# A row of zeros in a place of its own, two groups of keys ahead of the fill, and the fill behind the keys' loads

## The chip, the cores and the metric

One core of one Trainium2 chip runs the whole kernel in one launch. The metric is the device time of one execution in microseconds; the time before is 2405.3 us, the median of three runs (2400.01 to 2408.94).

The engines are called as in the profile: PE (matrix products), DVE (vectors), ACT (activations), POOL (GpSimd), SP (the engine that issues most of the transfers). Each runs its own instructions in order, and transfers issued by SP lie in SP's queue in order too.

## What is computed

Two layers of a graph network over 1250 nodes with 512 channels and 40000 edges. Only the first attention matters here. Each edge has a source, a destination and eight biases, one for each head:

```python
s = jnp.einsum('ehd,ehd->eh', q[src], k[dst]) / np.sqrt(D) + att_bias
m = jax.ops.segment_max(s, src, num_segments=n)
p = jnp.exp(s - m[src])
denom = jax.ops.segment_sum(p, src, num_segments=n)
alpha = p / jnp.where(denom[src] == 0, 1.0, denom[src])
agg = jax.ops.segment_sum(alpha[:, :, None] * v[dst], src, num_segments=n)
```

Behind it stand a linear attention over all nodes ("mix") that is added to the first, a feed-forward part, an attention with experts, a graph convolution over the same edges, a second linear attention, and a product-key layer.

## The kernel before

The kernel makes the sparse attention a dense one. A table in DRAM, `adj`, has one row of nine numbers for each pair of source and destination, 1280 x 1280 rows: for each head the sum of the exponentials of the biases of all edges between the two nodes, and how many such edges there are. With it, the attention is computed as a dense one whose exponentials are multiplied by the table (one slab of 128 sources at a time, `load_tile`, L667).

The table is made in three steps.

1. *The fill.* `zeros` (L227) writes zeros into the whole table: one transfer from SP's queue (L229) that reads one short row of zeros in SBUF, `zrow`, again and again, 59.0 MB in all, and one small transfer for some spare rows behind the table (L234). The row `zrow` is set by a memset on POOL (L498). It takes its memory from the pool "fold", under the tag `fwT`, which later holds weights.
2. *The groups of edges.* The key of an edge is source x 1280 + destination. Keys lie in columns of 128 edges, 313 columns. The columns are turned on PE, copied to SBUF by DVE (L275, two buffers) and stored in DRAM (`key_d`, three transfers on ACT's queue, L276). From there `load_keys` (L314, the transfer is L317, on SP's queue) brings nine columns, copied to all partitions, for each group of six columns. The pool of these loads has `KAHEAD` buffers. For each group DVE compares keys with keys (L332 and L342), PE adds up the weights of equal keys (L324), and DVE makes the sums (L349) and the indices (L355) of two batches of three columns.
3. *The scatters.* For each column one indirect transfer with addition (L358), issued by POOL, adds its rows into the table: 313 of them. The scatters come behind the fill, since they add into the same table, and a scatter comes behind those of the batch before last.

`scatter_edges` is a generator: each `pump(1)` writes down the instructions of one group between those of the mix attention. Its first step loads `KAHEAD` groups of keys and calls `zeros`, with the loads that are to land ahead of the fill: those of the keys and those in `early` (the node features and the mix attention's first weights and rows). The fill is then the last entry of `early`; some later loads are told to come behind it. There is one pump behind the first norms (L514), and within the loop over the ten node tiles one at t = 4 and one at t = 9 (L533). Then follow three, twenty, three and ten more by tiles and chunks (L553, L580, L592, L601), more with the projections of the sparse attention (L647, L652), and the rest of the groups at L653.

The order on each engine is made by a scheduler from these lines, with priorities by program order; SBUF comes from pools whose memory is used again when a pool is closed. The pool "edgetmp", which holds the edge weights `wgt`, is closed at L306, and pools that are opened later take its memory, with waits for its last readers. The casts of the weights into `w3` (L297, L299) are such readers.

Of the kernel before, what the change touches and what calls it, by code (L numbers as in the profile page):

```python
# [11 lines left out]
F32 = mybir.dt.float32  # L12
# [10 lines left out]
P = 128  # L23
N = 1250
NP = 1280
NT = NP // P
TAIL = N - (NT - 1) * P
C = 512
KC = C // P
# [9 lines left out]
CH = H + 1  # L39
NKEY = NP * NP  # L40
NROW = NKEY + (G + 1) * P
BIG = 1.0e30
LOWEST = -3.0e38
KAHEAD = 3
WSHIFT = 40.0
CHUNKS = ((0, 512), (512, 512), (1024, 256))
GROUPS = ((0, 4), (4, 4), (8, 2))
# [20 lines left out]
def tile_gps_layers(ctx: ExitStack, tc: tile.TileContext, a, out):  # L68
    nc = tc.nc
# [6 lines left out]
    def ps_mm(shape=(P, 512), name="mm"):  # L76
        return psum.tile(list(shape), F32, tag="mm", bufs=3, name=name)
# [4 lines left out]
    def ps_tr(shape=(P, 512), name="tr"):  # L82
        return psum.tile(list(shape), F32, tag="tr", bufs=2, name=name)
# [68 lines left out]
    def norm_stats(pool, x_t, eps, name):  # L152

        st = pool.tile([P, 6], F32, tag="ln_st", name=name + "st")
        nc.vector.bn_stats(st, x_t)
        mv = pool.tile([P, 2], F32, tag="ln_mv", name=name + "mv")
        nc.vector.bn_aggr(mv, st)
        return mv[:, 0:1], rsqrt(pool, mv[:, 1:2], [P, 1], eps, name)
# [27 lines left out]
    def node_mm(ps, xT, t, w, rows=P):  # L186

        mm(ps[:rows], [(xT[:, c, t * P:t * P + rows], w[:, c, :]) for c in range(xT.shape[1])])

    def nodes_of(t):  # L190
        return TAIL if t == NT - 1 else P
# [9 lines left out]
    adj = dram.tile([NROW, CH], F32, name="adj")  # L201
    key_d = dram.tile([EC, P], F32, name="key_d")
# [17 lines left out]

    s_edge = ctx.enter_context(ExitStack())
    pe = s_edge.enter_context(tc.tile_pool(name="edge", bufs=1, side="right"))
    pkr = s_edge.enter_context(tc.tile_pool(name="edgekr", bufs=KAHEAD, side="right"))
    s_tmp = ctx.enter_context(ExitStack())
    ptmp = s_tmp.enter_context(tc.tile_pool(name="edgetmp", bufs=1, side="right"))

    def zeros(zrow, inputs):  # L227

        ld = nc.sync.dma_start(  # L229
            adj[0:NKEY, :].rearrange("(p r) c -> p (r c)", p=P).rearrange("p (a f) -> p a f", f=1800),  # L230
            zrow[:, None, :].to_broadcast([P, NKEY * CH // P // 1800, 1800]))
        for x in inputs:
            tc.add_manual_dep(ld.ins, x.ins.name, SYNC, reason="inputs come first")
        nc.sync.dma_start(adj[NKEY:NROW, :].rearrange("(p r) c -> p (r c)", p=P), zrow[:, :(G + 1) * CH])  # L234
        return ld
# [30 lines left out]
    if whole < EC:  # L266
        nc.vector.tensor_tensor(keyrel[:, whole:], key[:, whole:], spare[:, :EC - whole], op=OP.subtract)


    for c0 in range(0, EC, P):  # L270
        cn = min(P, EC - c0)
        ps = ps_tr((P, P))
        nc.tensor.transpose(ps[:cn, :], key[:, c0:c0 + cn], ident)
        kt = ptmp.tile([P, P], F32, tag="kt", name="kt", bufs=2)
        nc.vector.tensor_copy(kt[:cn], ps[:cn, :])  # L275
        nc.scalar.dma_start(key_d[c0:c0 + cn, :], kt[:cn])  # L276


    mx = pe.tile([P, H], F32, name="mx")
# [28 lines left out]
    scattered, early = [], []  # L308

    def scatter_edges():  # L310
# [3 lines left out]
        def load_keys(c0):  # L314
            cn = min(G + B, EC - c0)
            kr = pkr.tile([P, (G + B) * P], F32, name="kr")
            ld = nc.sync.dma_start(  # L317
                kr[:, :cn * P],
                bass.AP(tensor=key_d.tensor, offset=key_d.offset + c0 * P, ap=[[0, P], [1, cn * P]]))
            return kr, ld  # L320
# [45 lines left out]
            scattered.append(cur)  # L366

        keys = [load_keys(c0) for c0 in range(0, KAHEAD * G, G)]
        early.append(zeros(zrow, [ld for _, ld in keys] + early))
        keys = [kr for kr, _ in keys]  # L370
        even = None
        for c0 in range(0, EC, G):
# [29 lines left out]
            yield  # L402

    edges = scatter_edges()

    def pump(n):
        for _ in range(n):
            next(edges, None)
# [85 lines left out]
    with (tc.tile_pool(name="mix", bufs=1) as pm, tc.tile_pool(name="mixw", bufs=2) as pw,  # L494
          tc.tile_pool(name="fold", bufs=1) as pfold):
        products = weight_products(pfold)
        zrow = pfold.tile([P, KC, C], F32, tag="fwT", name="zrow").rearrange("p c o -> p (c o)")[:, :1800]
        nc.gpsimd.memset(zrow, 0.0)  # L498
        nc.vector.memset(xn[:, NT - 1, :], 0.0)
        for t in range(NT):  # L500
            n = TAIL if t == NT - 1 else P
# [4 lines left out]
        def row(name):  # L506
            return rows[:, MIX_ROWS.index(name), :]
# [16 lines left out]
        for t in range(NT):  # L524
            ps = ps_mm()
            node_mm(ps, xnT, t, wk)
            nc.vector.tensor_tensor(kp[:, t, :], ps, bke, op=OP.add)
            nc.vector.tensor_scalar_max(kp[:, t, :], kp[:, t, :], eps)
            ps = ps_mm()
            node_mm(ps, xnT, t, wv)  # L530
            nc.vector.tensor_tensor(va[:, t, :, :D], ps.rearrange("p (h d) -> p h d", h=H),
                                    row("mix_bv").rearrange("p (h d) -> p h d", h=H), op=OP.add)
            if t in (4, 9):  # L533
                pump(1)

        kv = pm.tile([P, KC, 2, D + 1], F32, name="kv")
# [56 lines left out]
        for t in range(NT):  # L593
            ps = ps_mm()
            node_mm(ps, hid, t, w2)
            f = pw.tile([P, C], F32, tag="f", name="f")
# [20 lines left out]
    with tc.tile_pool(name="gqkv", bufs=2) as pq:  # L617
# [5 lines left out]
        for t in range(NT):  # L623
            z = pq.tile([P, C], F32, tag="z", name="z")
            m, r = norm_stats(pq, xn[:, t, :], 1e-5, "lnz")
# [226 lines left out]
    def node_norm(pool, t, x_t, eps, name):  # L852

        st = pool.tile([P, 6], F32, tag="nn_st", name=name + "st")
        nc.vector.bn_stats(st, x_t)
        mv = pool.tile([P, 2], F32, tag="nn_mv", name=name + "mv")
        nc.vector.bn_aggr(mv, st)
        w = pool.tile([P, 1], F32, tag="nn_w", name=name + "w")
        nc.vector.tensor_scalar_add(w, mv[:, 1:2], eps)
        s = pool.tile([P, 1], F32, tag="nn_s", name=name + "s")  # L860
        nc.scalar.activation(s, w, AF.Sqrt)
        r = pool.tile([P, 2], F32, tag="nn_r", name=name + "r")
        nc.vector.reciprocal(r[:, 0:1], s)
        nc.vector.tensor_scalar(s, r[:, 0:1], r[:, 0:1], w, op0=OP.mult, op1=OP.mult)
        nc.vector.tensor_scalar(s, s, -0.5, 1.5, op0=OP.mult, op1=OP.add)
        nc.vector.tensor_scalar(r[:, 0:1], r[:, 0:1], s, None, op0=OP.mult)
        nc.vector.tensor_scalar(r[:, 1:2], mv[:, 0:1], r[:, 0:1], -1.0, op0=OP.mult, op1=OP.mult)
        return r

    with tc.tile_pool(name="gff", bufs=1) as pf, tc.tile_pool(name="gffw", bufs=2) as pw:  # L870
# [33 lines left out]
        hTs, early = {}, {}  # L904
        with tc.manual_schedule(engines={nc.tensor.engine, nc.vector.engine, nc.scalar.engine}):
            for t in range(NT + 2):
                if t < NT:
# [7 lines left out]
                    r = node_norm(pw, t, X[:, t, :], 1e-5, "lnf")  # L915
# [24 lines left out]
            for c, (c0, cn) in enumerate(CHUNKS):  # L940
                n = cn // P
                for k, t in enumerate(range(c0 // P, c0 // P + n)):
# [4 lines left out]
                    r = nodes_of(t)  # L947
# [675 lines left out]
    keys = pp.tile([P, 2, 2, NKEYS], F32, name="keys")  # L1623
# [392 lines left out]
```

## Time and profile before

| what | us |
|---|---|
| median of three runs | 2405.3 |
| the profiled execution | 2407.57 |
| its span, first to last instruction | 2405.8 |
| busy in the span: PE | 1982.2 (82%) |
| busy in the span: DVE | 1511.2 (63%) |
| busy in the span: ACT | 811.5 (34%) |
| busy in the span: POOL | 695.8 (29%) |
| the fill, from issue to landing | 146.0 |
| the scatters, first start to last start | 196.7 to 790.5 |
| landing of a load of keys, shortest, median, longest | 3.6, 4.1, 5.6 |
| mean granted clock of PE | 0.904 of full speed |

The share of busy time is a mean over stages that have different limits: the edge stage (up to about 795 us), the sparse attention (to about 1160), and all the rest. A line of a timeline has the start, the duration, the engine, the line of the kernel and the operation; in brackets stand the idle time of the engine just ahead of it and what ended that. "SPq" is SP's instruction queue: its instructions issue transfers, and one that can't yet be issued holds all that are behind it.

### The profile page before, as it was taken

Reading aid. Unit: us, or ns where it says so; the run is one execution under the profiler, and the core shown is the slowest. Engines: PE = TensorE matmul, PEld = TensorE weight load, DVE = VectorE, ACT = ScalarE, POOL = GpSimd, SP = SyncE. Lnnn points to the kernel's source line nnn. Section 1 sums busy time; section 2 is a strip of 40 time slices with the busy share of each in tenths; the row PEclk is TensorE's granted clock in tenths of the full one; section 3 lists DMA queues with packets and bytes.
Section 4 is the critical chain, followed back from the end, with each engine's and each line's share of the span. In section 5 each row is a group of like instructions: output and inputs, shape, how many; then the busy total and the mean of one; then the engine's idle time right before and its main releaser. Section 6 shows DMA issues by size and latency. Waiting matters only on the chain.

```text
span 2405.8 us, 29769 instructions
## 1 busy us (share of the span) xinstructions
PE 1982.2 (82%) x10588; PEld 1179.4 (49%) x10588; DVE 1511.2 (63%) x4838; ACT 811.5 (34%) x1530; POOL 695.8 (29%) x448
## 2 busy tenths in 40 slices
PE   3994898965980499999899999999999999978953
PEld 1453665522440266666544546667445445555521
DVE  8526798599760399999651546655222242589998
ACT  1000111103200277677441166665111132244653
POOL 2006888888888100000000000000000000036665
PEclk9996898965995699999999999999899999989975
DMA  6999565545532665665330100001300101000000
GB/s 259 418 417 286 108 129 125 94 88 122 106 32 3 232 222 188 233 216 194 127 132 26 59 21 1 1 1 31 135 27 27 35 5 66 23 22 10 10 9 17
DMA packets 134336, 255.79 MB, mean 106 GB/s; under 512 B 51757, under 2 KB 90086, under 8 KB 132524
## 3 DMA queue, kind: packets, MB, share of 16 engines
q1 hardware_dynamic: 83728, 240.93, 27.2%
q0 software_dynamic: 46512, 8.02, 7.4%
q10 hardware_dynamic: 3948, 4.95, 0.6%
q8 instruction: 83, 1.36, 0.2%
q14 instruction: 65, 0.53, 0.1%
HBM read 161.05 MB, written 92.80 MB: 106 GB/s over the span
## 4 chain that ended last, share of the span: by engine, by line
PE 45%; DVE 12%; ACT 6%; DMA 2%; issue 1%; SPq 0%; ACTq 0%; DVEq 0%
PE mm L184 21%; PE one L747 4%; PE sc L698 4%; ACT wT L738 3%; PE ag L1400 2%; PE sc L1079 2%; PE av L1133 2%; PE one L737 2%; PE one L1120 2%; DVE sc L1760 2%; DVE ix L1701 1%; DVE ix L1710 1%; DVE rest L1713 1%; DVE v L1707 1%; DVE ex L727 1%
## 5 line engine op out<-in xcount | busy, mean ns | idle before, releaser
L358 POOL DMA_INDIRECT adj<-tot,idx x313 | 499.4, 1595 | 243.1 <-DMA adj<-zrow 147.1
L727 DVE SCALAR_TENSOR_TENSOR ex<-ex,slab 128x1280 f32<-128x1280 f32 x80 | 197.1, 2504 | 0.1
L1331 DVE SCALAR_TENSOR_TENSOR X<-mm,gate,X 128x512 f32<-128x512 f32 x80 | 60.0, 750 | 199.8 <-PE mm L184 199.7
L698 PE MATMUL sc<-kT,q 64*128 64x512 f32 (+1 forms) x480 | 103.6, 555 | 99.0 <-DMA q<-q_d 83.5
L332 DVE SCALAR_TENSOR_TENSOR eq<-kr,key,upto 128x128 bf16<-128x128 f32 (+2 forms) x313 | 145.7, 475 | 48.4 <-PE even L324 25.8
L342 DVE TENSOR_SCALAR_CACHE_REDUCE eqx<-kr,key 128x384 bf16<-128x384 f32 (+1 forms) x312 | 175.7, 599 | 0.0
L1269 POOL MEMSET padded<- 128x128 f32 x3 | 0.5, 204 | 540.2 <-DVE faT L1154 540.2
L738 ACT COPY wT<-one 128x512 f32<-128x512 f32 (+1 forms) x240 | 116.0, 517 | 92.2 <-PE one L737 87.6
L737 PE MATMUL one<-ident,ex 128*128 128x128 f32 x800 | 126.0, 286 | 25.5 <-ACT wT L738 20.6
L184 PE MATMUL mm<-w,hT 128*128 128x512 f32 (+1 forms) x320 | 146.0, 608 | 0.0
L184 PE MATMUL mm<-faT,w 128*128 128x512 f32 (+1 forms) x384 | 140.3, 519 | 0.7 <-ACT bs L1153 0.7
L708 DVE CUSTOM_DVE_ANT_0 ex<-sc,none 128x1280 f32<-128x1280 f32 x80 | 115.8, 1486 | 12.9 <-PE sc L698 11.8
L698 PEld LDWEIGHTS sc<-kT,q 64*128 64x128 f32 x480 | 46.4, 193 | 148.2 <-issue 129.4
L737 PEld LDWEIGHTS one<-ident,ex 128*128 128x128 f32 x800 | 84.7, 141 | 68.4 <-ACT wT L738 48.9
L1093 DVE CUSTOM_DVE_ANT_0 ex<-sc,cmask 128x512 f32<-128x512 f32 (+3 forms) x144 | 72.9, 560 | 66.7 <-PE sc L1079 66.6
L324 PEld LDWEIGHTS <-eq 128*128 128x128 bf16 x625 | 43.4, 102 | 135.5 <-DVE eq L332 91.8
L720 ACT ACTIVATE ex<-ex,low 128x1280 f32<-128x1280 f32 x80 | 104.8, 1361 | 9.9 <-DVE low L713 9.9
L184 PEld LDWEIGHTS mm<-faT,w 128*128 128x128 f32 x384 | 73.4, 192 | 67.1 <-issue 66.1
L684 POOL DMA_DIRECT2D deg_d<-cnt x10 | 8.4, 838 | 336.3 <-ACT attT L754 312.8
L747 PE MATMUL one<-wT,gva 128*64 128x128 f32 x1600 | 101.7, 285 | 3.6 <-ACT wT L738 2.0
L1325 ACT ACTIVATE hT<-mm,cols 128x512 f32<-128x512 f32 (+1 forms) x48 | 29.0, 608 | 218.9 <-PE mm L184 218.9
L184 PEld LDWEIGHTS mm<-w,hT 128*128 128x128 f32 (+1 forms) x320 | 61.6, 193 | 76.8 <-issue 76.8
(493 smaller groups left out, 4155.0 us busy)
## 6 DMA issues: line engine op xcount, KB each, us to landing
adj<-zrow SPq DMA_DIRECT2D x1, 57600.0 KB, 146.0
slab<-adj SPq DMA_DIRECT2D x10, 5760.0 KB, 17.4
kr<-key_d SPq DMA_DIRECT2D x51, 576.0 KB, 4.1
cnt_d<-cnt SPq DMA_DIRECT2D x10, 640.0 KB, 3.0
deg_d<-cnt POOLq DMA_DIRECT2D x10, 640.0 KB, 7.3
adjT<-cnt_d SPq DMA_DIRECT2D x5, 1280.0 KB, 10.7
adj<-tot,idx POOLq DMA_INDIRECT x313, 3.2
fw<-in_L_ffn_W SPq DMA_DIRECT2D x8, 512.0 KB, 3.9
```

Source lines behind the costliest of these rows:

```text
L184: nc.tensor.matmul(ps, lhsT=l, rhs=r, start=i == 0, stop=i == len(pairs) - 1)
L332: nc.vector.scalar_tensor_tensor(eq[:, :n], kr[:, k0 * P:k0 * P + n], key[:, c0 + c:c0 + c + 1], upto[:, B - 1 - c:, :].rearrange("p c x - ...
L342: nc.vector.tensor_scalar(eq[:, :n * P], kr[:, k0 * P:(k0 + n) * P], key[:, c0 + c:c0 + c + 1], None, op0=OP.is_equal, op1=OP.add, accum_o ...
L358: st = nc.gpsimd.indirect_dma_start(out=adj, out_offset=bass.IndirectOffsetOnAxis(ap=idx[:, c:c + 1], axis=0), in_=tot[:, c, :], in_offset ...
L698: nc.tensor.matmul(sc[e][:, d0:d0 + dn], lhsT=q[half(e), m, :], rhs=kT[half(e), m, d0:d0 + dn], start=True, stop=True)
L708: nc.vector.tensor_tensor_reduce(out=ex, in0=sc[e][:, :NP], in1=none, scale=-0.125, scalar=-LOWEST, op0=OP.add, op1=OP.min, accum_out=low[ ...
L720: nc.scalar.activation(exs[e], exs[e], AF.Exp, bias=low[:, e:e + 1], scale=-1.0)
L727: nc.vector.scalar_tensor_tensor(exs[e], exs[e], 1.0, sl[:, :, hd], op0=OP.mult, op1=OP.mult, accum_out=den[:, hd:hd + 1])
L737: nc.tensor.transpose(ps[:, k, :], weights[t, m][e][:, (d0 + k) * P:(d0 + k + 1) * P], ident)
L738: nc.scalar.copy(wT[:, d0:d0 + dn, :], ps[:, :dn])
L747: nc.tensor.matmul(av[half(e), 0, :], lhsT=va[:, d, hd * D:(hd + 1) * D], rhs=turned[e][:, d, :], start=d == 0, stop=d == NT - 1)
L1093: nc.vector.tensor_tensor_reduce(out=exs[e][:, d0:d0 + dn], in0=sc[k][e][:, :dn], in1=cmask[:, NP - n + d0:NP - n + d0 + dn], scale=-0.125 ...
```

## The change

The row of zeros gets a place of its own in the pool "edge", which is opened ahead of all edge work, and its memset stands there, among POOL's first instructions. It has 1600 elements instead of 1800, and the fill names 9216 rows instead of 8192. Two groups of keys are loaded ahead of the fill instead of three, and their pool has two buffers. The fill waits for the three stores of the keys and for `early`, and no longer for the loads of the keys. Of the two pumps in the loop over the node tiles one is left, at the last tile; that group of edges is written down in the last step (L653) instead.

```diff
-KAHEAD = 3
+ZROW = 1600
+KAHEAD = 2
...
     pe = s_edge.enter_context(tc.tile_pool(name="edge", bufs=1, side="right"))
+    zrow = pe.tile([P, ZROW], F32, name="zrow")
+    nc.gpsimd.memset(zrow, 0.0)
     pkr = s_edge.enter_context(tc.tile_pool(name="edgekr", bufs=KAHEAD, side="right"))
...
         ld = nc.sync.dma_start(
-            adj[0:NKEY, :].rearrange("(p r) c -> p (r c)", p=P).rearrange("p (a f) -> p a f", f=1800),
-            zrow[:, None, :].to_broadcast([P, NKEY * CH // P // 1800, 1800]))
+            adj[0:NKEY, :].rearrange("(p r) c -> p (r c)", p=P).rearrange("p (a f) -> p a f", f=ZROW),
+            zrow[:, None, :].to_broadcast([P, NKEY * CH // P // ZROW, ZROW]))
...
+    key_stores = []
...
-        nc.scalar.dma_start(key_d[c0:c0 + cn, :], kt[:cn])
+        key_stores.append(nc.scalar.dma_start(key_d[c0:c0 + cn, :], kt[:cn]))
...
-        early.append(zeros(zrow, [ld for _, ld in keys] + early))
+        early.append(zeros(zrow, key_stores + early))
...
         products = weight_products(pfold)
-        zrow = pfold.tile([P, KC, C], F32, tag="fwT", name="zrow").rearrange("p c o -> p (c o)")[:, :1800]
-        nc.gpsimd.memset(zrow, 0.0)
...
-            if t in (4, 9):
+            if t == NT - 1:
                 pump(1)
```

As the scheduler lays it out, SP's queue then has two key loads, the fill and its small second transfer, two key loads, the weights of L554 and L555, and only then the row of L556 (`gnn_b2`), which stood ahead of the fill. Each later key load keeps its place among SP's transfers. In DVE's order the one reader of `gnn_b2` (L557) moves from the fill's time to behind the fifth group of edges. On POOL only the memset moves, from behind the other early memsets to ahead of four of them.

## The prediction, made before the changed kernel ran

> **What bounds the kernel now.** I read the page's costliest groups first, then the stages, the timelines of SP's and POOL's queues, SP's waits, and the chain at the end of the edge stage. The group of scatters names the place:
>
> ```profile
> L358 POOL DMA_INDIRECT adj<-tot,idx x313 | 499.4, 1595 | 243.1 <-DMA adj<-zrow 147.1
> ```
>
> 313 scatters are busy for 499.4 us, and one single wait before them, for the fill of the table, is 147.1 us. The busy time of each engine by stages (PE, PEld, DVE, ACT, POOL; then granted clock, DMA share, GB/s):
>
> ```profile
> 50.00:196.00 146.00, 117.18 (x445) 64.84 (x445) 55.38 (x196) 7.56 (x23) 0.00 (x0) 0.87 1.01 412
> 196.00:693.00 497.00, 396.81 (x2507) 246.85 (x2508) 416.70 (x1946) 77.61 (x183) 416.47 (x260) 0.84 0.58 119
> 693.00:795.00 102.00, 22.05 (x52) 9.50 (x50) 4.96 (x8) 0.00 (x0) 82.90 (x54) 0.62 0.24 3
> ```
>
> From 50 to 196 the DMA engines are full with the fill; from 196 to 693 POOL scatters; from 693 to 795 only POOL scatters, and PE and DVE have nearly nothing left. POOL's timeline (start, duration, and what ended the idle time before it) gives the two ends of that run, and the row of zeros before it:
>
> ```profile
> 47.95 1.60 POOL L498 MEMSET zrow<- 128x1800 f32 x1 [35.84 <-DVE ln0r L149]
> ...
> 196.70 1.78 POOL L358 DMA_INDIRECT adj<-tot,idx  x1 [147.15 <-DMA adj<-zrow]
> ...
> 790.51 1.54 POOL L358 DMA_INDIRECT adj<-tot,idx  x1 [0.30 <-issue]
> ```
>
> The chain that ended last goes on from the last scatter into the attention: nothing of later stages starts before it.
>
> ```profile
> 790.51 3.52 DMA adj<-tot,idx
> ...
> 794.97 17.42 DMA slab<-adj
> ...
> 812.46 2.46 ACT cnt L682
> ```
>
> So the end of the scatters sets the time of all that follows (2405.8 - 790.5 = 1615 us, untouched by the diff). A scatter comes every 1.85 us (1.545 + 0.30): 312 steps are 577 us, and 196.7 to 790.5 is 593.8. Adding up what each step is above 1.85 gives 16.7; the run has no hole. It starts 1.1 us after the fill lands (49.6 + 146.0 = 195.6). **What moves the fill's end moves the kernel's end, as long as POOL never waits for DVE.** SP's waits and its queue tell why the fill starts at 49.6:
>
> ```profile
> SPq L229 <- POOL zrow L498: 14.9, 1, 14.9
> ...
> SPq L229 <- DMA kr<-key_d: 6.5, 1, 6.5
> ```
>
> ```profile
> 25.56 1.29 SPq L317 DMA_DIRECT2D kr<-key_d  x3
> 27.64 0.33 SPq L124 DMA_DIRECT2D gnn_b<-in_gnn_rows  x1
> 49.58 0.63 SPq L229 DMA_DIRECT2D adj<-zrow  x1
> 50.26 123.39 SPq L234 DMA_DIRECT2D adj<-zrow  x1
> 173.69 6.63 SPq L317 DMA_DIRECT2D kr<-key_d  x3
> ```
>
> SP stood at the fill from 28 on: 6.5 us for the third load of keys, then 14.9 us for the zeros' memset. From 34 to 48 the DMA share is 0.00. The memset stands in memory that the edge weights held, and these are last read by the cast of L297 (45.09 + 2.75 = 47.84).
>
> **The change, step by step.**
>
> *The zeros' row.* It has its own place and is set behind fold_g at about 2.9 us: the wait of 14.9 goes. The memset has 1600 elements instead of 1800: 1.60 x 1600/1800 = 1.42 us, now ahead of POOL's other memsets, which end at 12.11. DVE's first small operation stands beside them until just then:
>
> ```profile
> 4.06 8.07 DVE L518 TENSOR_SCALAR bqe<-cols 128x4 f32<-128x4 f32 x1 [2.07 <-DMA cols<-in_cols]
> ```
>
> So I add 1.42 us to DVE's early path, up to the key copies. The Trainium skill (SBUF — State Buffer, "Who interferes with whom") says that a DVE operation in a two-port mode and a GpSimd instruction hold a shared port pair exclusively, the second waiting for the first. That fits L518; by the page's one-instruction lock it would be free at 10.1, the end of the first memset, where the trace has 12.1.
>
> *What the fill waits for next.* The key stores and the inputs, instead of the key loads and the inputs. The queue's inputs sum to 9.4 MB, and the DMA engines had moved that much by 26.5 to 27 us. Of the key stores, the third copy stood at 25.59 in DVE because it waits until the first store frees its buffer, and was issued at 25.9. With DVE 1.42 later: 27.3. Its landing is not in the trace; the nearest rows are scatters at 2.9 to 3.4 and key loads at 3.6 to 5.6, another key store, beside the full input stream, took 9.4. I take 3.2, since by then the stream has drained: **the fill starts at 30.5**. Bounds: SP reaches it at 27.9; and at most 1.4 behind the 34.5 of the key loads that it waited for before: 36.
>
> *The fill itself.* 59.0 MB in either form, 9216 rows of 6400 bytes for 8192 of 7200. At 412 to 418 GB/s the engines are full, and the input stream with its 2 KB rows moved 432 between 20 and 26 us; so the row size costs nothing that I can see, and 146.0 stays. About 0.5 us is added for the tail of two key loads still in the rings at 30.5 (1.2 MB, issued by 27.9). End: 30.5 + 146.0 + 0.5 = 177.0, against 195.6: **18.6 us earlier**. The Trainium skill (DMA: Bandwidth & Descriptors, "How a descriptor splits into AXI transactions") says that pieces which don't start on 256 bytes cost an extra transaction: 6400 is a multiple of 256, 7200 isn't. A faster fill is among the rivals.
>
> *The third key group and gnn_b2* move behind the fill in SP's queue. gnn_b2's one reader, L557, moves in DVE's order behind the fifth group of edges, far behind that load. Three groups made 18 scatters ready ahead of the fill's end (33 us of POOL); two make 12: 12 x 1.85 = 22.2 us. After the fill, DVE started at 197.13, 1.5 us behind it, and had the next indices at 200.6, 5 us behind it. The 13th scatter is wanted 1.1 + 22.2 = 23.3 us behind it: 18 us to spare. I laid each index (L355) beside its scatter: the smallest lead of all 105 batches is 30.1 us, at the first batch behind the fill, then 32 growing to 67. One group less takes 11.1 off: never under 18. PE and DVE finish what is ahead of the fill's end at 175, with one group less and 1.4 more still about 175: before 177, so their 22 us of standing (DVE 174.5 to 197.1) shrink to some 4.
>
> *Two buffers.* In SP's order each key load keeps its slot and is released by the same event; it is only used one group earlier. For every load I set its issue + 4.6 against the start of the group before its own: 2.5 us to spare at 203.43, 0.6 at the tightest (issue 228.56, group at 233.71), 2.0 near 660, 6.2 through 480 to 560. With the slowest landing, 5.6, one group is 0.4 late, under a lead of 18. Cost: nothing.
>
> *One more group beside the scatters* (its DVE work was done during the fill). The scatters' excess over 1.85 is all ahead of 693, none from 700 to 790 with DVE idle: 16.7/50 = 0.3 us.
>
> Sum: 18.6 - 0.3 = 18.3 us off 2407.6, the profiled execution (span 2405.8 and 1.8 around it): 2389.3. That execution lies 2.3 above the median of 2405.3, so I predict **2387**.
>
> **Rivals.**
> - *The fill waits longer for the stores:* it starts at 36, gain 13: 2392. For it: a key store took 9.4 among the inputs. Against it: the share falls to 0.86 behind 26.
> - *A faster fill* by its other rows: at the best rate near it, the inputs' 432, instead of 418, it takes 146 x (1 - 418/432) = 4.7 us less: 2382. Against it: the engines read full at 418 already. (It is what that page's rule on 256 bytes would make of it.)
> - *The start runs dry:* the groups behind the fill come late, because the pre-fill work of PE ends later than 177. It must end 18 us later to cost anything; at 28 late, 10 are lost: 2397. Against it: PE's work there is one unbroken row of matmuls that ends at 175.
> - *Slower: two buffers starve POOL.* If a key load lands too late in each group, DVE's period of 10.0 us (480 to 560) grows past POOL's 11.9. That takes a landing above 6.2 + 4.6 + 1.9 = 12.7 us. At 14 the period is 13.2: 1.3 x 50 = 65, less the lead of 19 = 46, less the 18.6 gained: 27 slower, 2432. Against it: landings are 3.6 to 5.6.
> - *It doesn't do what it says:* the fill still waits for something at 49: 2405. The row is the first tile of its pool and its memset names no wait in POOL's instruction list; little speaks for it.
>
> **How the numbers follow.** Forecast 0.72; late stores 0.10; faster fill 0.05; dry start 0.05; no move 0.04; starving 0.04. Half a per cent, about what a measurement of this kernel can tell from no change, is 12 us: 2393.3. Faster holds the forecast, the faster fill and half of the late stores, 0.82; same the other half, the dry start and no move, 0.14; slower 0.04. The range goes from a start at 27.9 with the faster fill (2405.3 - 21.2 - 4.7 = 2379) to the late start (2392), widened by 1 and 4 for the spread of the runs (2400 to 2409): 2378 to 2396.
>
> **What would show it.** The fill's DMA issued at 30.5 (27.9 to 36) with a landing near 146; the first scatter near 178 and the last near 772; POOL's wait for the fill about 163 us, since POOL now stands from about 13.5; no scatter waiting on an index; DVE's wait for keys at the fill's end about 4 us instead of 22.6; everything from the first slab on 18 us earlier and otherwise the same. Wrong would be: a fill above 150 us; holes in the run of scatters; key loads that DVE waits for later on.

## The result, and the profile after

The changed kernel takes 2387.25 us, the median of five runs (2384.58 to 2394.72), against 2405.3 for the kernel before (five runs, 2398.38 to 2408.94): a ratio of 0.9925 with an interval of 0.9909 to 0.9941. The forecast was 2387. The profiled execution has a span of 2384.9, 20.9 less than before's.

The group of scatters with its single wait, and the stages, cut at the same events as before's (PE, PEld, DVE, ACT, POOL; granted clock, DMA share, GB/s):

```profile
L362 POOL DMA_INDIRECT adj<-tot,idx x313 | 500.4, 1599 | 260.4 <-DMA kr<-key_d 163.8
```

```profile
32.00:177.00 145.00, 126.22 (x439) 67.42 (x437) 61.96 (x181) 7.43 (x23) 0.00 (x0) 0.92 1.01 412
177.00:675.00 498.00, 395.01 (x2488) 246.41 (x2489) 414.65 (x1925) 77.45 (x183) 417.03 (x260) 0.82 0.59 122
675.00:777.00 102.00, 27.96 (x100) 12.08 (x98) 15.26 (x62) 0.00 (x0) 83.38 (x54) 0.66 0.26 3
```

The three stages have kept their lengths within 1 us, and all of them lie earlier. The third has one more group's work in it (PE 28.0 against 22.1, DVE 15.3 against 5.0). POOL's busy time is the same (500.4, before 499.4), and its wait is longer only because POOL has stood since 13.7. The page of the profile now names a key load as what ended that wait. The scatters wait for several transfers, and the profile has no landing of the fill in this run; in experiment nine, where it has one, the fill lands 144.7 us behind its issue and the first scatter starts 1.3 us later. POOL's timeline shows the ends of the run, and SP's queue and wait show what the fill starts behind:

```profile
2.87 1.44 POOL L225 MEMSET zrow<- 128x1600 f32 x1
...
177.50 1.78 POOL L362 DMA_INDIRECT adj<-tot,idx  x1 [163.82 <-DMA kr<-key_d]
...
772.98 1.55 POOL L362 DMA_INDIRECT adj<-tot,idx  x1 [0.30 <-issue]
```

```profile
22.46 0.82 SPq L321 DMA_DIRECT2D kr<-key_d  x2
31.57 0.64 SPq L232 DMA_DIRECT2D adj<-zrow  x1
32.26 113.18 SPq L237 DMA_DIRECT2D adj<-zrow  x1
```

```profile
SPq L232 <- DMA key_d<-kt: 8.1, 1, 8.1
```

The fill is issued at 31.57 instead of 49.58, 18.0 earlier; the first scatter comes 19.2 earlier, the last 17.5 earlier (790.51 to 772.98). The chain behind the last scatter has the same links, with the slab's load 17.47 us long (17.42 before):

```profile
772.98 3.10 DMA adj<-tot,idx
776.32 0.59 SPq L678
777.07 17.47 DMA slab<-adj
794.68 2.46 ACT cnt L684
```

From the last scatter to the end it is 1611.9 us, 3.4 less than before. It can't be put down to the change: the same kernel profiled again took 1618.9 there.

### The profile page after: what moved, and what is told of

Same layout as the page of the kernel before. It is cut to its first block, busy times and chain, and to the rows that moved or that the text cites. A ratio compares the mean times of both kernels' runs of the same rounds, so it can differ in the third digit from the quotient of the medians.

```text
span 2384.9 us, 29756 instructions
## 1 busy us (share of the span) xinstructions
PE 1981.0 (83%) x10588; PEld 1177.0 (49%) x10588; DVE 1510.2 (63%) x4838; ACT 810.7 (34%) x1530; POOL 697.0 (29%) x448
## 4 chain that ended last, share of the span: by engine, by line
PE 57%; DVE 24%; ACT 7%; DMA 5%; issue 3%; POOL 3%; SPq 1%; DVEq 0%; ACTq 0%; POOLq 0%
PE mm L185 30%; PE sc L700 4%; DVE eqx L346 4%; PE one L749 4%; POOL adj L362 3%; ACT wT L740 3%; DVE eq L336 3%; PE one L739 2%; PE ag L1402 2%; PE sc L1081 2%; PE av L1135 2%; PE one L1122 2%; DVE sc L1762 2%; DMA kr<-key_d 1%; DVE ix L1703 1%
## 5 line engine op out<-in xcount | busy, mean ns | idle before, releaser
L362 POOL DMA_INDIRECT adj<-tot,idx x313 | 500.4, 1599 | 260.4 <-DMA kr<-key_d 163.8
L1333 DVE SCALAR_TENSOR_TENSOR X<-mm,gate,X 128x512 f32<-128x512 f32 x80 | 60.0, 750 | 196.8 <-PE mm L185 196.7
L739 PE MATMUL one<-ident,ex 128*128 128x128 f32 x800 | 127.5, 288 | 23.8 <-ACT wT L740 20.1
```

The costliest lines, as they stand in the source:

```text
L362: st = nc.gpsimd.indirect_dma_start(out=adj, out_offset=bass.IndirectOffsetOnAxis(ap=idx[:, c:c + 1], axis=0), in_=tot[:, c, :], in_offset ...
L739: nc.tensor.transpose(ps[:, k, :], weights[t, m][e][:, (d0 + k) * P:(d0 + k + 1) * P], ident)
```

## Experiments

Below, "the fill" is the time of its issue, "first" and "last" are the starts of the first and last scatter, and "the rest" is the span behind the last. Before has 49.6, 196.7, 790.5 and 1615.3, after has 31.6, 177.5, 773.0 and 1611.9. Theory A was the prediction's: the row's old memory holds the memset, the memset holds the fill, and the fill's landing starts a run of scatters that never waits.

**One: the place alone.** Before, with the row in its own place and three buffers of keys; these leave room for 576 elements only.

```diff
+    zrow = pe.tile([P, 576], F32, name="zrow")
+    nc.gpsimd.memset(zrow, 0.0)
...
-        zrow = pfold.tile([P, KC, C], F32, tag="fwT", name="zrow").rearrange("p c o -> p (c o)")[:, :1800]
-        nc.gpsimd.memset(zrow, 0.0)
```

> The kernel before with one edit: the row of zeros in its own place in the pool of the edges (576 elements, as more does not fit beside three groups of keys; the fill then has 25600 rows of 2304 bytes). Three groups of keys, the fill waiting for their loads, and the pumps stay as they were. Theory A (the memset's wait for the edge weights was what held the fill): the fill is issued when the third key load has landed, 34 to 35 us instead of 49.6, lasts 145 to 146, and the whole kernel takes 15 us less: 2390, ratio 0.994. Theory B (the two groups and the wait for the stores did it): the fill still comes near 49, 2405, ratio 1.000. If rows of 2304 bytes were slower to write, the fill would last longer than 146 and take that off the gain.

2404.52 (12 runs, 2397.18 to 2418.58), ratio 0.9994 (0.998 to 1.0008). The fill starts at 33.77, 15.8 earlier, but the first scatter comes 154.4 behind it instead of 147.1, at 188.19, and the last at 784.36. So the wait is gone and half of its worth is spent: the fill moves 392 GB/s between 60 and 150 us, against 417 in before. The fill comes when Theory A says, but the time misses its 2390. The last scatter is 6.2 us earlier in the trace, and the median shows no gain clear of the noise.

**Two: the old place.** After, with the row's tile and memset back in "fold".

```diff
-    zrow = pe.tile([P, ZROW], F32, name="zrow")
-    nc.gpsimd.memset(zrow, 0.0)
...
+        zrow = pfold.tile([P, KC, C], F32, tag="fwT", name="zrow").rearrange("p c o -> p (c o)")[:, :ZROW]
+        nc.gpsimd.memset(zrow, 0.0)
```

> The changed kernel with one edit undone: the row of zeros in its old place, in memory that the edge weights held. Two groups of keys, the wait for the stores, and the pump at the last tile stay. Theory A: the memset waits for the last cast of the edge weights, which ends at 44.4 in the trace of the changed kernel; with 1.4 us of memset the fill is issued at about 46, 14.5 later than in the changed kernel: 2387 + 14.5 = 2402, ratio to before 0.998. Theory B: the fill comes at 31 to 32, 2387, ratio 0.993.

2394.76 (2390.5 to 2397.64), ratio 0.9951 (0.9938 to 0.9964). The first link of Theory A falls here. POOL sets the row at 10 us, without a wait, and the fill is issued 1.2 us later than in after:

```profile
10.05 1.43 POOL L500 MEMSET zrow<- 128x1600 f32 x1
```

First 178.51, last 771.74. The median is 7.5 us above after's and no execution lies below 2390.5; the trace, which is of the fastest execution, has 1.2 us of it in the fill's start and none at the last scatter, so most of that difference is open. In this layout the old place is no obstacle; the only other edit that moves memory is the third key buffer. Theory B: the third buffer pushed the row onto the memory of the edge weights, and giving it up is enough.

**Three: two buffers alone.** Before with `KAHEAD = 2`, nothing else.

> The kernel before with one number changed: two buffers of keys in place of three; the zeros' row stays in its old place (1800 elements), the fill still names the keys' loads. Theory B, formed from the run with the old place: the third buffer is what held the row, since it pushed the row's memory onto memory that the casts of the weights still read; without it the row's memset comes in the stretch of memsets at 10 us, and the place of its own adds nothing. It expects the fill to be issued when the keys' loads have landed, at 33 to 34 us (33.77 where the row had its own place and three loads stood ahead), the first scatter 147 us later at 180.5 to 181.5, the last at 774 to 776, and 2389 to 2393 us on the kernel before's 2406.9. Rival C: the place itself matters, the memset waits on, the fill comes after 44 us, the first scatter after 191, and the time is 2403 to 2407.

2397.28 (12 runs, 2391.79 to 2415.43), ratio 0.998 (0.996 to 1.0001). In the trace Theory B holds, and rival C falls. The row's memset and the first scatter:

```profile
10.04 1.60 POOL L498 MEMSET zrow<- 128x1800 f32 x1
```

```profile
180.88 1.78 POOL L358 DMA_INDIRECT adj<-tot,idx  x1 [167.27 <-DMA kr<-key_d]
```

The fill starts at 34.16, 15.4 of the 18.0 us earlier. What Theory B says of the memory has to be put more exactly, by the addresses in the compiled programs, which no profile shows. The row's own bytes don't lie on the edge weights, neither here nor in before. In before it is the pool "fold" that reaches 832 bytes of each partition into the pool "edgetmp", onto a tile that isn't the weights. The row is the first tile of "fold", and its memset is told to wait for readers of other tiles of "edgetmp" too, the weights' last cast (L297) among them. With one buffer of keys less, "edgetmp" lies 4608 bytes higher, the two pools don't meet, and the wait is gone.

But the time is above the forecast, and three of the twelve runs lie at 2413 to 2415. The profiled execution is one of them, and its rest is 1634.2. The loss sits directly behind the scatters, in TensorE's first scores: here they start 39.1 us behind the last scatter (779.51), in after 8.6. The first line is of after, the second of this kernel:

```profile
781.57 4.30 PE L700 MATMUL sc<-kT,q 64*128 64x512 f32 x12 [78.34 <-DMA q<-q_d]
```

```profile
818.65 4.64 PE L698 MATMUL sc<-kT,q 64*128 64x512 f32 x12 [109.04 <-DMA q<-q_d]
```

The load of q, 256 KB, is issued by ACT and the slab (5.76 MB) by SP, behind SP's load of the next q; both wait for the last scatters. The first three lines are of after, the others of this kernel:

```profile
776.30 0.61 ACTq L678 DMA_DIRECT2D q<-q_d  x1
776.32 0.59 SPq L678 DMA_DIRECT2D q<-q_d  x1
777.07 0.97 SPq L672 DMA_DIRECT2D slab<-adj  x2
```

```profile
782.64 0.59 SPq L676 DMA_DIRECT2D q<-q_d  x1
782.88 0.61 ACTq L676 DMA_DIRECT2D q<-q_d  x1
783.45 0.92 SPq L670 DMA_DIRECT2D slab<-adj  x2
```

In after ACT issued it 0.77 ahead of the slab, and it landed in 5 us. Here it was issued 0.57 ahead of the slab and took some 36 us, as long as two slabs. In the seven traces in which ACT issued it just ahead of SP's own load of q (by 0.02 to 0.04 us) the scores came early; in the four in which it came 0.24 to 0.26 behind that, they came once early (two), once 18 us behind the issue (one), and twice 36 us behind (three, and four's 576). The 18 us cost one nothing: its rest is 1612.4, since q landed about when the first slab did. The 36 us went with a rest of 1634.2 in three and 1630.5 in four. I call that Theory Q; experiment five tests it.

**Four: the row's length.** After with `ZROW = 576`, and then with 1440.

> The changed kernel with one number changed: the zeros' row is 576 elements long (2304 bytes), and the fill repeats it 200 times in place of 72. Theory R: the length of the row sets the fill's rate. In the run with the place alone the rate was 391 to 393 GB/s from 50 to 180 us, against 418 with 1600 elements. It expects the fill to be issued at 31.6 us, 154 us until the first scatter, so 185 to 186.5, the last scatter at 780 to 783, and 2393 to 2397 us. Rival: the third load of keys made the fill of that run slow, not the row; then 146 us, first scatter at 177.5, 2387 us.

2398.37 (10 runs, 2395.36 to 2419.79), ratio 0.9982 (0.996 to 1.0003). The fill starts at 31.54, first 186.80, which is 155.3 behind it: the row's length it is, and the third key load of the first experiment has no part in it. The time is above the forecast's 2393 to 2397, and two of the ten executions lie at 2412 and 2420; the profiled one is one of them.

> The changed kernel with a row of 1440 elements (5760 bytes, 22.5 times 256) in place of 1600 (6400 bytes, 25 times 256); the fill repeats it 80 times in place of 72. So far: 2304 bytes (9 times 256) took 154.6 us from the fill's issue to the first scatter, 6400 bytes 145.2 to 145.9, 7200 bytes (28.1 times 256) 146.7 to 147.1. If the rate goes by the number of rows alone, 1440 lies at 146.3 (0.53 ns for each of the rows, from 2304 and 6400), and 7200 should have been at 145.3, which it wasn't. If a row that is no multiple of 256 bytes pays for its last piece (the Trainium skill, DMA: Bandwidth & Descriptors, states a rule of that kind), 1440 lies above 147.1. Forecast: 147 to 149 us, first scatter at 178.5 to 180.5, 2388 to 2392 us.

One time, 2397.35; the fill at 34.13, and 149.3 until the first scatter. Both are above the forecast, in part since the fill came 2.6 us later than in after. With the DMA engines at a share of 1.01 to 1.03, the rates between 60 and 150 us are 392 GB/s for 2304 bytes (both kernels), 408 for 5760, 418 for 6400 (after) and 417 for 7200 (before, and three). So of the change's 72 instead of 64 repeats nothing is felt, and a short row is dear. The Trainium skill (DMA: Bandwidth & Descriptors, "How a descriptor splits into AXI transactions") has one transaction more for what is left over of a piece that is no multiple of 256 bytes. The 408 of 5760 bytes, 22.5 times 256, agrees with it; the 417 of 7200 bytes, 28.1 times 256, does not, and 2304, 9 times 256, is the slowest. It is not what orders these four, and what does is open.

**Five: the load of q ahead of the slab.** The kernel of three (two buffers alone), with q in SP's queue.

```diff
+            q = pw.tile([P, KC, P], F32, tag="q", name="q")
+            nc.sync.dma_start(q, q_d[:, :, t * P:(t + 1) * P])
             sl = pslab.tile([P, NP, CH], F32, tag="slab", name="slab")
...
-            q = pw.tile([P, KC, P], F32, tag="q", name="q")
-
-            queue = nc.sync if t else nc.scalar
-            queue.dma_start(q, q_d[:, :, t * P:(t + 1) * P])
```

> The kernel before with two buffers of keys in place of three, as in the run with two buffers alone, and one more edit behind the edge stage: the first small load of the attention stage (q, 256 KB) goes ahead of the slab in SP's queue, in place of a queue of its own on ACT. Theory Q: what spreads the times of the kernels with the old place, with the short row and with two buffers alone is that load. Where ACT issued it 0.02 to 0.04 us ahead of SP's (before, after), it landed 4 to 5 us later and TensorE began beside the slab's transfer; where ACT issued it 0.25 us behind, it landed after one slab or after both, up to 36 us later. With the load ahead of the slab, Theory Q expects no execution above 2400, a median of 2389 to 2392 us, the first scatter at 180 to 181.5 and TensorE's first scores within 10 us of the last scatter in the profile. Rival: the spread comes from the granted clock or from the edge stage; then the median stays at 2394 to 2398 and some executions lie above 2404.

2396.38 (11 runs, 2389.14 to 2401.7), ratio 0.9955 (0.9942 to 0.9967). The scores start 7.1 us behind the last scatter, and no run lies at 2404 or above, where four of the twelve did; two lie above the 2400 that Theory Q gave as the limit (2400.98 and 2401.7). That half of Theory Q holds, as far as the traces of two such executions (three's and four's) and these runs, on another chip, can show it: the late load is what put the outliers there. The median did not come down to the 2389 to 2392 that it expected, so the load does not explain the bulk of the runs. Two buffers, with q moved, give 10.7 us by this median. What keeps it from the 15 that the fill's start is earlier, I can't say in full: in the profile first is 181.11 and last 778.24, 12.3 earlier, with a run of 597.1 against 593.8, and the rest took 1617.4.

**Six: no wait for the keys' stores.** After, with `zeros(zrow, early)`.

> The changed kernel without the fill's wait for the three key stores: it waits for the inputs alone. In the changed kernel the fill was issued at 31.6, behind 8.1 us of waiting that the trace puts down to a key store, and the DMA engines were nearly empty from 30.7 to 33. Theory A (the stores end last): the fill is issued when the inputs have landed, 27 to 30, its rows follow the key loads without a hole, the end of the fill and the kernel's end come 2 to 3 us earlier: 2384.5, ratio to before 0.9915. Rival (the inputs' last rows land with the stores): nothing moves, 2387, 0.9925.

2387.54 (2385.55 to 2390.11), ratio 0.9924 (0.9911 to 0.9936). The fill starts at 28.16, 3.4 earlier, first 174.69, last 768.60, 4.4 earlier; the rest took 1615.3, 3.4 more than in after, and the time is the same. The gain in the edge stage is real in the trace and not larger than the rest's own spread (below).

**Seven: one group ahead.** After with `KAHEAD = 1`, and without the pump of L535, whose group is written down at the end.

> The changed kernel with one group of keys ahead and one buffer for the key loads; the second pump ahead of the fill's end is taken out, and its group is written down in the last step. Theory A (the key loads ahead only have to keep DVE in front of POOL): 6 scatters are ready at the fill's end, 11 us, the first group behind it is ready 5 us behind it, so the lead falls from 17.7 to about 7; with one buffer each group waits 4 to 5 us for its load, DVE's period grows from 10 to about 12 and more against POOL's 11.1 to 11.9, the lead is used up at the dip near 450 us (25 us deep in the changed kernel), and POOL stands for 15 to 60 us in all: 2405 to 2450. Rival (POOL bounds with time to spare, so the number ahead is of no account): the fill comes 1.4 us earlier with one load less ahead of it, 2386.

2431.73 (2428.22 to 2432.47), ratio 1.01 (1.0085 to 1.0115). First is at 175.91, last at 797.62. DVE's waits for keys between 177 and 800 us, in after first (total, times, longest), then here, and a hole in POOL's run here:

```profile
DVE eq L336 <- DMA kr<-key_d: 12.0, 3, 10.0
```

```profile
DVE eq L336 <- DMA kr<-key_d: 107.8, 40, 9.3
```

```profile
459.05 1.55 POOL L362 DMA_INDIRECT adj<-tot,idx  x1 [0.30 <-issue]
474.64 1.67 POOL L362 DMA_INDIRECT adj<-tot,idx  x1 [14.04 <-DVE tot L353]
```

DVE stands 40 times for a group's keys, and the run's excess over 1.85 us a step is 44.6 instead of 18.3. That is the rival "two buffers starve POOL", one buffer further on. Of the 44.7 us by which its span (2429.6) exceeds after's, the scatters have 24.6 (773.0 to 797.6) and the rest 20.1 (1632.0): q was issued at 801.04, behind the slab's 800.66, and the scores started 36 us later.

**Eight: one group ahead of the fill, but two buffers.** After, with the fill between the two key loads.

```diff
+        early.append(zeros(zrow, early))
         keys = [load_keys(c0) for c0 in range(0, KAHEAD * G, G)]
-        early.append(zeros(zrow, key_stores + early))
```

> The changed kernel with the fill issued ahead of the second load of keys, not behind it, and without the wait for the keys' stores: only one group of keys is loaded when the fill starts. Theory A: the second group's keys are what covers the edge stage behind the fill; they now arrive when the fill has landed and DVE has no second group compared, so after the first group's 6 batches of scatters (about 11 us) POOL waits for an index: first scatter at 174 to 177, a hole of 10 to 30 us in the first 40 us of the scatters, the last scatter at 782 to 800, and 2396 to 2415 us. Rival: the load's packets pass beside the fill's at a share of the DMA engines, land early, and nothing is lost: 2384 to 2389 us.

2391.08 (2388.56 to 2394.91), ratio 0.9933 (0.9912 to 0.9955). The hole that Theory A expected is not there, and its rival's early landing isn't either; the time is above the rival's 2384 to 2389, with a rest of 1619.2. DVE got the second group's keys only behind the fill:

```profile
176.48 0.35 DVE L336 SCALAR_TENSOR_TENSOR eq<-kr,key,upto 128x128 bf16<-128x128 f32 x1 [8.01 <-DMA kr<-key_d]
```

First is at 174.27, and six ready scatters (11.1 us) last until the next indices, which came at 180.0: the lead is 6.0 at its smallest, and POOL never waited (last 770.80). So one group ahead is enough, with 6 us left. What seven lost in its run of scatters, it lost by its one buffer.

**Nine: fewer rows ahead of the fill.** The kernel of six, with two of the eight constant rows of the mix attention loaded ahead of the fill and six behind it. Then the same with q as in five.

```diff
-        rows = rows_bc(pm, a["mix_rows"], len(MIX_ROWS), name="mixrows", into=early)
+        rows = rows_bc(pm, a["mix_rows"][0:2], 2, name="mixrows", into=early)
...
+        rest = rows_bc(pm, a["mix_rows"][2:8], 6, name="mixrest", into=later)
+        tc.add_manual_dep(later[0].ins, early[-1].ins.name, SYNC, reason="the zeros come first")
```

> The changed kernel without the wait for the keys' stores, and with only the first two of the eight rows of the mixing stage's constants (0.5 of 2.1 MB in SBUF) loaded ahead of the fill, the other six behind it; all is computed. Theory A: the fill starts when the queues ahead of it have run dry, so a load moved behind it is time saved: fill issued at 26 to 28 us, first scatter at 172 to 174.7, the last at 766 to 769, 2382 to 2385 us. Rival: as where the wait for the stores alone was dropped (fill at 28.2, last scatter 4.4 us earlier, time 2387.5 on 2387.3), the edge stage ends earlier and the stages behind it give it back, and the time is 2386 to 2389.

2383.62 (six runs, 2378.49 to 2386.11), ratio 0.9914 (0.9893 to 0.9935). The fill starts at 25.46, first 171.47, 146.0 behind it, last 768.65. This is the fastest version; on the same chip the changed kernel took 2389.15:

> The changed kernel again, beside the others on their chip: 2385 to 2390 us, fill issued at 31 to 32 us, first scatter at 177 to 178.

It had 2383.43 to 2394.33, six runs, ratio 0.9936 (0.9914 to 0.9958). The two intervals overlap, but the trace has first 6.7 and last 3.3 us earlier.

> The version that the runs point to: the changed kernel, without the wait for the keys' stores, with two of the eight constant rows ahead of the fill and six behind it, and with the attention stage's first q load ahead of the slab in SP's queue. All is computed. Theory A and Q: first scatter at 171 to 172 and last at 765 to 769 as in the run with the rows split, first scores within 10 us of the last scatter, 2381 to 2385 us and no execution above 2390. Rival: the q load on SP costs more than the lottery it removes, since it delays the slab by its own transfer: 2385 to 2388.

2388.22 (2386.04 to 2389.76), ratio 0.9921 (0.9905 to 0.9936). The edge stage is the same (171.33, 766.22), the rest 1618.8, and the slab is issued 4.6 us behind the last scatter, 3.9 in nine. The rival's 2385 to 2388 is the nearer; where q landed early anyway, moving it brought nothing that these runs show.

**The spread of the rest.** In executions with an early q it is 1611.2 to 1619.2, in the same kernel 1611.9 and 1618.9. Set against the last scatter, the two traces of that kernel run level (within 0.2 us) to 86 us behind it, are 2.9 apart at 408 and 5.4 at 1064, with a mean granted clock of 0.906 and 0.903. The cause I leave open; a gain of 3 us in the edge stage can't be read from one median beside it.

## Why the prediction was right

The chain was right, and its sizes have errors that cancelled. That the median fell within 0.3 us of the forecast is luck beyond that: the five executions lie from 2384.6 to 2394.7, the span of the profiled one fell by 20.9 where the sum has 18.3, because the rest took 3.4 us less, and the kernel measured again took 2389.15, which is 15.0 below the kernel before on that chip (2404.16).

- *The chain.* The end of the scatters sets the time, the fill's landing sets their start, and all behind moves along: 19.2 at the first, 17.5 at the last scatter, for 18.6 and 18.3 forecast. In every kernel but seven's the run of scatters is 593 to 599 us long, wherever it starts.
- *The wait of 14.9 goes: right in size, incomplete in cause.* I put it down to the place alone, and to memory that the edge weights had held. Three and two show that the third buffer held the row, by the pools that meet and not by the row's own bytes; either edit by itself removes the wait. In the traces they belong together only by room: with three buffers the own place takes 576 elements, and these cost 7.3 us of fill in one and 9.3 in four. The medians of the three kernels with the old place and two buffers (2394.76, 2397.28, 2396.38) stay 7 to 10 us above after's, and the traces don't say why in full.
- *DVE 1.42 later: failed.* POOL's early memsets end at 13.68 instead of 12.11, as I added them up. But DVE had another operation beside them, and it came free at 12.27, in before at 12.13:

```profile
3.91 0.42 DVE L520 TENSOR_SCALAR bqe<-cols 128x4 f32<-128x4 f32 x1 [1.92 <-DMA cols<-in_cols]
...
5.85 6.42 DVE L261 CAST key<-src_i 128x313 f32<-128x313 int32 x1 [0.96 <-DMA src_i<-in_src]
```

  L520, held for 8.07 us in before, takes 0.42 and ends as the row's own memset does (4.33 and 4.31). The cast of the keys, which took 0.31 in before, is held over the ends of two memsets (11.49 and 11.66), to about that of a third (12.09), and goes on while the last one runs (12.04 to 13.68). The Trainium skill's lock of one instruction (SBUF — State Buffer, "Who interferes with whom") would have let it go at 11.5; my "until POOL has done" would have been 13.7. The trace of the cast agrees with neither.
- *The third store at 27.3, landing 3.2: both wrong, opposite signs.* The three stores were issued within 16.94 to 23.59, 4 us earlier than I had them, since the first store, which frees the third's buffer, landed earlier and the third copy came at 22.78 (25.59 before). But SP waited for them until 31.5, a landing of some 8 us, not 3.2: the DMA engines read 0.98 from 28 to 30 us, full for 3 us longer than I took. I had the 9.4 of another store beside the full stream in hand and set it aside for a stream that I believed drained. Net, the fill starts 1.1 late, within the bounds.
- *The fill, 146.0 and 0.5: 1.7 too long.* From issue to first scatter it is 145.9, where the sum makes 147.6 of it (146.0, 0.5 and 1.1 to the first scatter) and before has 147.1; the two kernels' rates are 418 and 417. With the 1.1 of the late start this leaves the first scatter 0.6 ahead of the forecast. The run of scatters, 1.4 longer than the 594.1 of the sum, then takes the last one 0.8 behind it.
- *The cover: right.* No scatter waits for an index; the smallest lead is 17.7, where I had 18. DVE's wait at the fill's end is 10.0 and not 4, since the work ahead of it ended at 169, not 175:

```profile
178.97 0.35 DVE L336 SCALAR_TENSOR_TENSOR eq<-kr,key,upto 128x128 bf16<-128x128 f32 x1 [10.03 <-DMA kr<-key_d]
```

- *Two buffers cost nothing: right.* Behind that first wait DVE waits 2.0 us for keys in all. The run is 595.5 against 593.8. With two buffers it lies between 593.1 (four) and 598.6 (three), with three buffers at 593.8 and 596.2 (one), so the 1.7 can't be put down to them.
- *The rivals.* Late stores (31.6, not 36), a faster fill (1.2, not 4.7) and a dry start did not come. Starving needs one buffer, not two. "It doesn't do what it says" had the right question in it: another edit than the one named first frees the row as well.

## What to carry to other kernels

Where a wait comes from memory that is used again, look at every edit that moves the pool's bounds, not only at the tile that waits: here a smaller buffer count alone took the wait away. The start of a bulk transfer that a serial run waits for moves that run, so what stands ahead of it in the queue (stores to be landed, constants that are needed later) can be weighed one by one, as in nine; the 3.4 us that six gained there didn't show in its time. And a small load that shares the engines with a large one should be issued well ahead of it; in three's profiled execution a quarter of a microsecond went with a loss of some 20 us.

## What the runs showed of the hardware

- The rate of the fill, which repeats one row from SBUF into DRAM, was lowest for the shortest row: 392, 408, 418 and 417 GB/s for 2304, 5760, 6400 and 7200 bytes, all at a DMA share of 1.01 to 1.03.
- A load of 256 KB issued 0.77 us ahead of a slab of 5.76 MB landed in 5 us; issued 0.5 to 0.6 us ahead, it landed in 5, 18 or 36 us; issued 0.4 us behind the slab (seven), in 36.
- A small store beside a full input stream landed after some 8 us; key loads in the edge stage of before took 3.6 to 5.6.
